# Attention logits: from TensorE matmuls to a copy of k through memory, a VectorE transpose and a ScalarE leaky ReLU

## Chip, core and metric

One core of one Trainium2 chip runs the whole program. The metric is device time in microseconds. Before the change it is 1596.43 us, the median of three runs (1595.44 to 1596.8).

## The reference

128 graphs, each with 128 nodes of 256 features (float32) and its own 128x128 adjacency. Layer 0 is a graph convolution, layer 1 graph attention with 8 heads. The change is in the lines of `logits` and `masked`:

```python
h  = relu(layernorm(x))                       # layer 0
x  = x + adj @ (h @ weight) + bias
h2 = relu(layernorm(x))                       # layer 1
fp = (h2 @ fc_w + fc_b)                       # 8 heads of 256
q, k = fp @ q_w + q_b, fp @ k_w + k_b         # one number per node and head
logits = q + transpose(k)                     # 128 x 128 per head
masked = leaky_relu(logits + (1 - adj) * -1e9, 0.01)
attn = softmax(masked)
out = sigmoid((attn @ fp) @ fp_w + fp_b + h2)
x = x + out
```

## The kernel before

**Groups and slots.** A group is GB = 4 graphs; there are 32. A hand-written program puts each engine's instructions in order. One group is 44 slots on TensorE: four units (two pairs of graphs times two halves of the heads), each with the 11 entries of ORDER (L590). A "g" entry multiplies the attention by h2 (`aggregate`, L559) into PSUM; a number m is the product of the combined term f[m] with a folded weight (`multiply`, L604), which for a unit stands 11 slots behind its g. `take` (L576 to L585) brings g out of PSUM: ScalarE copies f0, f1 and f3, VectorE makes f4 and f6, GpSimd f5 and f2. So unit 0's f4 is multiplied at slot 16, unit 2's f3 at slot 34. `combine` (L620 to L639) puts a pair's results together on VectorE.

**PLAN.** The list PLAN (L665) says after which slot other work is put into the engines' queues, as (slot, group relative to the current one, function). Each engine runs its own queue in order; an entry's slot fixes that order, and an engine can be ahead of TensorE's slot or behind. In the time of group g, group g+1 goes through its softmax, g+2 gets its second layer norm, its transposed h2 (`turn_h2_blocks`, L435) and q and k, and g+3 goes through layer 0: `first_a` (L372, copied out by ScalarE at L379) at slot 35, `first_b` (L388, with VectorE's add at L395) at slots 37 and 40. The statistics (L290, L291) and `rdev_both` (L302 on VectorE, L306 on GpSimd) follow; the normalization itself is a ScalarE ReLU with scale and bias per node (L324). Group g-1 gets its sigmoid (L652), `finish` (L656) and the store.

**Logits.** `make_qk` computes q and k of a group for all heads as rows: 32 rows for each graph, 8 of q, 8 of k, 16 empty (L459). `left` (L467) and `kr` (L469) hold these rows with ones put in, and `right` (L471, GpSimd) spreads `kr` over the heads, zero but for the own head. One matmul per graph and half of the blocks, with 32 rows in the contraction, then gives q + k for 128x512 at once in PSUM:

```python
nc.tensor.matmul(lp, lhsT=s["left"][ts(b, Q), :], rhs=s["right"][ts(b, Q), js],
                 start=True, stop=True)
```

`logits` (L486) runs at slots 1 and 4, four matmuls each. `masked` (L499) adds the mask on VectorE, from PSUM into the tile `attn`; `head_max` (L511) applies the leaky ReLU as max(0.01 a, a) and takes the negative maximum per head (L513). `exps` (L521) is one ScalarE Exp per head, with the maximum as bias and the sum read out. `normal` scales by the reciprocal (L529 on VectorE, L530 on GpSimd). `move` (L541) sends 32-row blocks of attn to other partitions, 16 DMAs a pair, all in SyncE's queue, and `turn` (L548) transposes them in 32x32 blocks on VectorE. SyncE's queue also holds the moves of h2 (L431), the loads (L67, L69, L77) and the output (L657). Matmuls write to the six PSUM buffers of ps_m.

Before the first group, a setup folds the weights and takes groups 0 and 1 through the same steps by hand; FIRST_PLAN adds what is missing in the first group.

Of the kernel before, what the change touches and what calls it, by code (L numbers as in the profile page):

```python
# [9 lines left out]
FP = mybir.dt.float32  # L10
# [8 lines left out]
H = 8  # L19
# [9 lines left out]
def gnn_then_gat_kernel(  # L29
# [31 lines left out]
    small = ctx.enter_context(tc.tile_pool(name="small", bufs=3))  # L61
    ps_m = ctx.enter_context(tc.tile_pool(name="ps_m", bufs=6, space=PSUM))
# [42 lines left out]
    mq = const.tile([P, 1], FP, name="mq")  # L105
    mk = const.tile([P, 1], FP, name="mk")
    lb = const.tile([P, 1], FP, name="lb")
    rb = const.tile([P, 1], FP, name="rb")
    heads = const.tile([P, H], FP, name="heads")
# [29 lines left out]
    cols = sp.tile([P, ROWS], FP, name="cols")  # L139
    ones = sp.tile([P, P], FP, name="ones")  # L140
# [6 lines left out]
    def setup_rows():  # L147
# [23 lines left out]
        nc.vector.tensor_tensor(heads, rows[:, 0:H], rows[:, H : 2 * H], ALU.add)  # L171
# [52 lines left out]
    def setup_bias():  # L224
# [253 lines left out]
    def logits(s, half, bs=range(GB)):  # L478
# [3 lines left out]
        js = ts(half, NB // 2)  # L482
        for b in bs:
            lp = ps_m.tile([P, NB // 2, H, Q], FP, name="logits", tag="m")
            s["l", half, b] = lp
            nc.tensor.matmul(  # L486
                lp,
                lhsT=s["left"][ts(b, Q), :],
# [309 lines left out]
    for half in range(2):  # L798
        n1_apply(s1, half)
# [153 lines left out]
```

## Time and profile before

| What | Value |
|---|---|
| median of the runs | 1596.43 us |
| the profiled execution: time, and its span | 1593.71 us, 1591.9 us |
| its mean granted TensorE clock | 0.987 |
| a steady stretch of 96 us (302 to 398): clock; busy PE, DVE, ACT, POOL | 1.00; 96.00, 82.96, 56.49, 70.50 us |
| DMA queue of SyncE: share of 16 engines | 35.4% |
| idle of VectorE before L499, put down to the logits | 137.3 us in 61 waits |
| idle of ScalarE before the Exp, put down to the maximum | 95.4 us in 65 waits |

The steady stretch is two groups and a little. A group of instructions is told by its line, engine and operation, output and inputs, then the shape, the count, the busy time in us and the mean of one in ns, and at the end the idle time of the engine before them with what ended it. A timeline row is its start in us, its length, and the same names. float32 matmuls leave two records each. PE is TensorE, DVE VectorE, ACT ScalarE, POOL GpSimd, SP SyncE.

### The profile page before, as it was taken

The numbers are of one execution on the slowest core, as the hardware profiler recorded it, in microseconds if no ns is written. First come the engines' busy times: TensorE is split into PE (matmuls) and PEld (weight loads), VectorE is DVE, ScalarE is ACT, GpSimd is POOL, SyncE is SP. The second block draws the span as 40 slices with busy tenths as digits, with TensorE's granted clock in tenths as the row PEclk, the third lists the DMA queues.
The fourth block names the chain that finished last, engine by engine and source line by source line (L and its number), as shares of the span: only waits on it lengthen the run. The fifth ranks groups of instructions, "written<-read, shape, count | busy, mean of one in ns | idle before, by whom it ended". The sixth has DMA issues, their size and how long they took to land.

```text
span 1591.9 us, 30601 instructions
## 1 busy us (share of the span) xinstructions
PE 1564.3 (98%) x10433; PEld 1229.5 (77%) x10433; DVE 1313.2 (82%) x2352; ACT 888.2 (56%) x2865; POOL 1112.5 (70%) x756
## 2 busy tenths in 40 slices
PE   7989999999999999999999999999999999999997
PEld 6667777877777877777777777887777787777776
DVE  5888888988888998888898888898888898887762
ACT  3554556665555665555666555666555666555551
POOL 2465778766678766677866677876667876667774
PEclk7899999999999999999999999999999999999999
DMA  5233334333334433333433333433333443323220
GB/s 179 53 81 87 84 90 100 91 83 92 90 82 98 98 89 84 90 79 97 102 88 86 87 80 95 102 91 83 90 91 82 99 96 86 89 71 78 70 67 27
DMA packets 236644, 139.44 MB, mean 88 GB/s; under 512 B 151860, under 2 KB 203464, under 8 KB 236232
## 3 DMA queue, kind: packets, MB, share of 16 engines
q1 hardware_dynamic: 236248, 137.16, 35.4%
q8 instruction: 82, 1.34, 0.4%
q14 instruction: 74, 0.61, 0.1%
q10 hardware_dynamic: 240, 0.33, 0.1%
HBM read 37.76 MB, written 16.78 MB: 34 GB/s over the span
## 4 chain that ended last, share of the span: by engine, by line
PE 93%; DVE 2%; DMA 1%; issue 1%; POOL 1%; ACT 1%; SPq 0%; POOLq 0%; DVEq 0%
PE acc L604 51%; PE g_ps L559 28%; PE x_ps L388 6%; PE logits L486 4%; PE ah_ps L372 3%; PE qk_ps L459 1%; DMA fpw<-in_L_gnn_fp_w_dram 1%; DVE attn L499 0%; ACT attn L521 0%; DMA b_bc<-in_L_gnn_bias_dram 0%; DVE attn L511 0%; DVE attnT L548 0%; DVE st L290 0%; DVE nmax L513 0%; ACT h L324 0%
## 5 line engine op out<-in xcount | busy, mean ns | idle before, releaser
L604 PEld LDWEIGHTS acc<-wts,f 128*128 128x128 f32 x7168 | 895.6, 192 | 296.1 <-issue 255.4
L604 PE MATMUL acc<-wts,f 128*128 128x128 f32 x7168 | 909.6, 276 | 3.9 <-ACT f L584 3.9
L559 PE MATMUL g_ps<-attnT,h 128*128 128x512 f32 x1024 | 529.4, 599 | 4.3 <-DVE attnT L548 4.3
L521 ACT ACTIVATE attn<-attn,nmax 128x128 f32<-128x128 f32 x1024 | 397.5, 391 | 96.2 <-DVE nmax L513 95.4
L582 POOL TENSOR_TENSOR f<-f,f 128x512 f32<-128x512 f32 x128 | 193.3, 1510 | 298.6 <-DVE f L580 294.1
L530 POOL TENSOR_TENSOR attn<-attn,total 128x1024 f32<-128x1024 f32 x128 | 277.8, 2170 | 40.9 <-DVE total L529 40.9
L584 ACT COPY f<-g_ps 128x512 f32<-128x512 f32 x128 | 73.6, 575 | 382.9 <-PE g_ps L559 231.3
L499 DVE TENSOR_TENSOR attn<-logits,mask 128x512 f32<-128x512 f32 x256 | 159.0, 683 | 137.3 <-PE logits L486 137.3
L511 DVE SCALAR_TENSOR_TENSOR attn<-attn 128x1024 f32<-128x1024 f32 x128 | 207.5, 1621 | 0.0
L585 POOL TENSOR_TENSOR f<-f,f 128x512 f32<-128x512 f32 x128 | 188.9, 1476 | 8.9 <-ACT f L584 3.9
L521 ACT ACTIVATION_READ_ACCUMULATOR attn<-attn,nmax 128x1 f32 x1024 | 193.1, 189 | 0.0
L548 DVE STREAM_TRANSPOSE attnT<-attnB 128x1024 f32<-128x1024 f32 x128 | 154.5, 1226 | 14.2 <-DMA attnB<-attn 13.8
L559 PEld LDWEIGHTS g_ps<-attnT,h 128*128 128x128 f32 x1024 | 155.8, 192 | 13.1 <-issue 10.1
L513 DVE TENSOR_REDUCE nmax<-attn 128x8 f32<-128x1024 f32 x128 | 156.2, 1220 | 4.4
L578 ACT COPY f<-g_ps 128x512 f32<-128x512 f32 x128 | 73.5, 574 | 115.5 <-PE g_ps L559 115.5
L648 POOL TENSOR_TENSOR z<-z,h 128x256 f32<-128x256 f32 x128 | 90.5, 727 | 51.7 <-DVE z L620 44.1
L388 PE MATMUL x_ps<-w_sb,ahT 128*128 128x256 f32 x512 | 121.0, 380 | 0.0
L620 DVE TENSOR_TENSOR z<-w,v 128x256 f32<-128x256 f32 (+1 forms) x128 | 116.2, 947 | 2.2
L388 PEld LDWEIGHTS x_ps<-w_sb,ahT 128*128 128x128 f32 x512 | 93.0, 191 | 11.0 <-issue 1.0
L576 ACT COPY f<-g_ps 128x512 f32<-128x512 f32 x128 | 73.6, 575 | 41.9 <-PE g_ps L559 40.7
L580 DVE TENSOR_TENSOR f<-g_ps,f 128x512 f32<-128x512 f32 x128 | 85.8, 670 | 8.2 <-PE g_ps L559 6.1
L581 DVE TENSOR_TENSOR f<-f,g_ps 128x512 f32<-128x512 f32 x128 | 86.5, 676 | 0.0
(95 smaller groups left out, 1444.6 us busy)
## 6 DMA issues: line engine op xcount, KB each, us to landing
attnB<-attn SPq DMA_DIRECT2D x1019, 64.0 KB, 2.0
xg<-in_x_dram SPq DMA_DIRECT2D x32, 512.0 KB, 4.1
out_dram<-z SPq DMA_DIRECT2D x31, 512.0 KB, 2.9
h2B<-h SPq DMA_DIRECT2D x480, 32.0 KB, 1.9
ag<-in_adj_dram SPq DMA_DIRECT2D x32, 256.0 KB, 4.7
agB<-in_adj_dram SPq DMA_DIRECT2D x120, 64.0 KB, 4.3
fcw<-in_L_gnn_fc_w_dram SPq DMA_DIRECT2D x2, 1024.0 KB, 7.2
fpw<-in_L_gnn_fp_w_dram SPq DMA_DIRECT2D x1, 2048.0 KB, 14.1
```

The source lines that it names most:

```text
L388: nc.tensor.matmul(op[:, bb, :], lhsT=s["ahT"][:, 2 * b2 + bb, c, :], rhs=w0_sb[:, c, :], start=(c == 0), stop=(c == NC - 1),)
L499: nc.vector.tensor_tensor(s["a", b // 2][:, js, b % 2], s["l", half, b], s["mask"][:, b, :] .rearrange("p (j c) -> p j c", c=Q)[:, js] .un ...
L511: nc.vector.scalar_tensor_tensor(a, a, 0.01, a, ALU.mult, ALU.max)
L513: nc.vector.tensor_reduce(nmax, a.rearrange("p j h c -> p h j c"), AX.XY, ALU.max, negate=True)
L521: nc.scalar.activation(a[:, :, h, :], a[:, :, h, :], AF.Exp, bias=s["nmax", b][:, h : h + 1], accum_out=s["total", b][:, h : h + 1],)
L530: nc.gpsimd.tensor_tensor(a, a, total.unsqueeze(1).unsqueeze(3).to_broadcast([P, NB, H, Q]), ALU.mult)
L548: nc.vector.transpose(aT.rearrange("p h (i r) -> p i h r", r=Q), s["ab", b // 2][:, :, b % 2])
L559: nc.tensor.matmul(u["g", b, c], lhsT=s["h2"][:, 2 * pair + b].rearrange("p j c q -> p (j c q)")[:, ts(c, P)], rhs=s["aT", 2 * pair + b][: ...
L582: nc.gpsimd.tensor_tensor(new(5), f[4], f[0], ALU.subtract)
L585: nc.gpsimd.tensor_tensor(new(2), f[1], f[5], ALU.subtract)
L604: nc.tensor.matmul(acc[:, slot, :], lhsT=u["f"][m][:, h, :], rhs=wt[m][:, half * HU + h, :], start=(half == 0 and h == 0 and m in FIRST), ...
L620: nc.vector.tensor_tensor(o, a, b, ALU.add)
```

## The change

`left`, `right` and `logits` go, with their PLAN entries. `make_qk` adds the bias to the rows (`qk`). `turn_qk` transposes them on TensorE, so that nodes lie on partitions, copies k and q out on VectorE and stores k (128 x 32 numbers) to a buffer in memory. `load_k` reads it back four times, each into 32 partitions, so that each block of 32 partitions holds all of k. `spread` is VectorE's 32x32 transpose with an input in which each number is repeated 32 times, so that its output holds k along the row in every partition. `masked` is that and then one mask add over 128x1024, in place in SBUF. `leaky` is one ScalarE Prelu per head, with q as its bias and slope 0.01; `head_max` keeps just the maximum. The PLAN moves: the softmax steps start at slot 0, the Exp run in eights, the moves of attn are split (8, 8, 6, 10) around the store and the loads of k, make_qk stands at slot 24 instead of 30, add_b0 behind finish instead of before it, and the output's DMA is split off from finish (`store`). In the setup the same steps take the place of the logits of groups 0 and 1.

```diff
--- before.py
+++ after.py
@@ -59,6 +59,7 @@
     gp = ctx.enter_context(tc.tile_pool(name="group", bufs=2))
     at = ctx.enter_context(tc.tile_pool(name="attention", bufs=2))
     small = ctx.enter_context(tc.tile_pool(name="small", bufs=3))
+    mem = ctx.enter_context(tc.tile_pool(name="mem", bufs=2, space=bass.MemoryType.DRAM))
     ps_m = ctx.enter_context(tc.tile_pool(name="ps_m", bufs=6, space=PSUM))
     ps_o = ctx.enter_context(tc.tile_pool(name="ps_o", bufs=1, space=PSUM))
 
...
@@ -232,12 +230,9 @@
                 start=(kk == 0),
                 stop=(kk == NC - 1),
             )
-        bias = sp.tile([P, 1], FP, name="bias")
         both = sp.tile([P, 1], FP, name="both")
         nc.vector.scalar_tensor_tensor(both, mq, qkb[:, 0:1], bp, ALU.mult, ALU.add)
-        nc.vector.scalar_tensor_tensor(bias, mk, qkb[:, 1:2], both, ALU.mult, ALU.add)
-        nc.vector.scalar_tensor_tensor(lb, bias, mq, mk, ALU.mult, ALU.add)
-        nc.vector.scalar_tensor_tensor(rb, bias, mk, mq, ALU.mult, ALU.add)
+        nc.vector.scalar_tensor_tensor(qk_bias, mk, qkb[:, 1:2], both, ALU.mult, ALU.add)
 
 
 
...
@@ -463,52 +457,63 @@
                     start=(c == 0),
                     stop=(c == NC - 1),
                 )
-        s["left"] = gp.tile([P, P], FP, name="left", tag="left")
-        nc.vector.tensor_scalar(s["left"], qk, mq, lb, ALU.mult, ALU.add)
-        kr = small.tile([P, P], FP, name="kr", tag="kr")
-        nc.vector.tensor_scalar(kr, qk, mk, rb, ALU.mult, ALU.add)
-        s["right"] = gp.tile([P, NB, H, Q], FP, name="right", tag="right", bufs=1)
-        nc.gpsimd.tensor_tensor(
-            s["right"],
-            heads.unsqueeze(1).unsqueeze(3).to_broadcast([P, NB, H, Q]),
-            kr.rearrange("p (j c) -> p j c", c=Q).unsqueeze(2).to_broadcast([P, NB, H, Q]),
-            ALU.mult,
-        )
-
-    def logits(s, half, bs=range(GB)):
-
-
-
-        js = ts(half, NB // 2)
-        for b in bs:
-            lp = ps_m.tile([P, NB // 2, H, Q], FP, name="logits", tag="m")
-            s["l", half, b] = lp
-            nc.tensor.matmul(
-                lp,
-                lhsT=s["left"][ts(b, Q), :],
-                rhs=s["right"][ts(b, Q), js],
-                start=True,
-                stop=True,
-            )
-
-    def masked(s, half, bs=range(GB)):
-        js = ts(half, NB // 2)
-        for b in bs:
-            if half == 0 and b % 2 == 0:
-                s["a", b // 2] = at.tile([P, NB, 2, H, Q], FP, name="attn", tag="attn", bufs=3)
-            nc.vector.tensor_tensor(
-                s["a", b // 2][:, js, b % 2],
-                s["l", half, b],
-                s["mask"][:, b, :]
-                .rearrange("p (j c) -> p j c", c=Q)[:, js]
-                .unsqueeze(2)
-                .to_broadcast([P, NB // 2, H, Q]),
-                ALU.add,
+        s["qk"] = gp.tile([P, P], FP, name="qk", tag="qk", bufs=1)
+        nc.vector.tensor_scalar(s["qk"], qk, qk_bias, None, ALU.add)
+
+    def turn_qk(s):
+
+
+        tp = ps_m.tile([P, GB, Q], FP, name="q_ps", tag="m")
+        nc.tensor.transpose(tp.rearrange("p b r -> p (b r)"), s["qk"], ident)
+        k = small.tile([P, GB, H], FP, name="k", tag="k", bufs=2)
+        nc.vector.tensor_copy(k, tp[:, :, H : 2 * H])
+        s["q"] = gp.tile([P, GB, H], FP, name="q", tag="q")
+        nc.vector.tensor_copy(s["q"], tp[:, :, 0:H])
+        s["k_mem"] = mem.tile([P, GB * H], FP, name="k_mem", tag="k_mem")
+        nc.sync.dma_start(s["k_mem"], k.rearrange("p b h -> p (b h)"))
+
+    def load_k(s):
+        s["kq"] = gp.tile([P, NB, GB, H], FP, name="kq", tag="kq")
+        for n in range(NB):
+            nc.sync.dma_start(
+                s["kq"][ts(n, Q)].rearrange("r j b h -> r j (b h)"),
+                s["k_mem"].rearrange("(j r) c -> r j c", r=Q),
+            )
+
+
+
+    def spread(s, b):
+
+        if b % 2 == 0:
+            s["a", b // 2] = at.tile([P, NB, 2, H, Q], FP, name="attn", tag="attn", bufs=3)
+        nc.vector.transpose(
+            s["a", b // 2][:, :, b % 2],
+            s["kq"][:, :, b].unsqueeze(3).to_broadcast([P, NB, H, Q]),
+        )
+
+    def masked(s, b):
+        spread(s, b)
+        a = s["a", b // 2][:, :, b % 2]
+        nc.vector.tensor_tensor(
+            a,
+            a,
+            s["mask"][:, b, :]
+            .rearrange("p (j c) -> p j c", c=Q)
+            .unsqueeze(2)
+            .to_broadcast([P, NB, H, Q]),
+            ALU.add,
+        )
+
+    def leaky(s, b, h0=0, nh=H):
+        a = s["a", b // 2][:, :, b % 2]
+        for h in range(h0, h0 + nh):
+            nc.scalar.activation(
+                a[:, :, h, :], a[:, :, h, :], AF.Prelu,
+                bias=s["q"][:, b, h : h + 1], alpha=0.01,
             )
 
     def head_max(s, b):
         a = s["a", b // 2][:, :, b % 2]
-        nc.vector.scalar_tensor_tensor(a, a, 0.01, a, ALU.mult, ALU.max)
         nmax = s["nmax", b] = small.tile([P, H], FP, name="nmax", tag="nmax", bufs=4)
         nc.vector.tensor_reduce(
             nmax, a.rearrange("p j h c -> p h j c"), AX.XY, ALU.max, negate=True
@@ -654,6 +659,9 @@
     def finish(s, b0, nb):
         bs = slice(b0, b0 + nb)
         nc.gpsimd.tensor_tensor(s["z"][:, bs], s["z"][:, bs], s["x1"][:, bs], ALU.add)
+
+    def store(s, b0, nb):
+        bs = slice(b0, b0 + nb)
         nc.sync.dma_start(
             out[GB * s["g"] + b0 : GB * s["g"] + b0 + nb].rearrange("b n d -> n b d"),
             s["z"][:, bs],
@@ -664,67 +672,71 @@
 
     PLAN = [
         (0, "u", take, 0, 0, 0),
-        (1, 1, logits, 0),
-        (1, 1, masked, 0),
+        (0, 1, masked, 0),
+        (0, 1, masked, 1),
+        (0, 1, leaky, 0),
         (2, 2, shift_both),
         (3, "u", take, 0, 1, 1),
         (3, 2, n2_apply, 0),
         (3, 2, n2_apply, 1),
         (3, 2, move_h2),
-        (4, 1, logits, 1),
-        (4, 1, masked, 1),
+        (4, 1, leaky, 1),
+        (4, 1, head_max, 0),
+        (5, 1, masked, 2),
         (6, "u", combine, -1, 4),
-        (6, 1, head_max, 0),
+        (7, "u", take, 0, 1, 0),
+        (7, 1, head_max, 1),
         (8, 4, begin),
         (8, 3, load_blocks),
-        (8, "u", take, 0, 1, 0),
         (9, "u", take, 0, 0, 1),
-        (9, 1, exps, 0, 0, 4),
-        (10, 1, head_max, 1),
-        (11, "u", take, 1, 0, 0),
+        (9, 1, exps, 0, 0, 8),
         (11, "u", combine, -1, 2),
         (11, -1, residual_b, 1),
-        (11, 1, exps, 0, 4, 4),
+        (11, "u", take, 1, 0, 0),
+        (11, 1, leaky, 2),
         (12, 0, turn, 2),
+        (12, 1, masked, 3),
         (12, 1, normal, 0),
-        (13, 1, exps, 1, 0, 1),
-        (13, 1, head_max, 2),
+        (13, 0, turn, 3),
         (14, "u", take, 1, 1, 1),
-        (14, 1, exps, 1, 1, 3),
-        (15, 1, exps, 1, 4, 4),
-        (16, 0, turn, 3),
-        (17, 1, normal, 1),
+        (14, 1, head_max, 2),
+        (14, 1, exps, 1, 0, 8),
         (17, "u", take, 1, 1, 0),
-        (17, 1, exps, 2, 0, 4),
-        (18, 1, exps, 2, 4, 2),
-        (19, 1, head_max, 3),
+        (18, 2, turn_h2_blocks),
+        (18, 1, normal, 1),
+        (18, 1, move, 0, range(8)),
         (20, "u", take, 1, 0, 1),
-        (20, 1, exps, 2, 6, 2),
-        (20, 1, move, 0),
+        (20, 1, leaky, 3),
+        (20, 1, head_max, 3),
+        (20, 1, exps, 2, 0, 8),
         (21, 0, residual_a, 0),
-        (22, 1, normal, 2),
         (22, "u", take, 2, 0, 0),
         (22, 1, exps, 3, 0, 4),
-        (24, 3, n1_apply, 0),
+        (24, 2, make_qk),
         (25, "u", take, 2, 1, 1),
+        (25, 1, normal, 2),
+        (25, 1, exps, 3, 4, 4),
+        (25, 3, n1_apply, 0),
         (25, 3, n1_apply, 1),
-        (26, 1, exps, 3, 4, 4),
-        (26, 2, turn_h2_blocks),
         (27, "u", combine, 1, 4),
+        (28, "u", take, 2, 1, 0),
+        (27, 2, turn_qk),
+        (28, 1, move, 0, range(8, 16)),
+        (28, 1, normal, 3),
         (28, 3, turn_blocks),
         (28, 4, n1_stats, 0),
-        (28, "u", take, 2, 1, 0),
         (28, 4, n1_stats, 1),
-        (28, 3, add_b0),
         (28, -1, sigmoid, 0, GB),
         (29, -1, finish, 0, GB),
-        (30, 1, normal, 3),
-        (30, 2, make_qk),
+        (29, 3, add_b0),
+        (30, 1, move, 1, range(6)),
         (31, "u", take, 2, 0, 1),
         (32, "u", combine, 1, 2),
         (32, 0, residual_b, 0),
         (33, "u", take, 3, 0, 0),
-        (33, 1, move, 1),
+        (34, 2, load_k),
+        (34, 1, move, 1, range(6, 16)),
+        (34, -1, store, 0, GB),
         (34, 1, turn, 0),
         (34, 1, turn, 1),
         (35, 3, first_a, 0),
@@ -741,7 +753,7 @@
         (43, 0, residual_a, 1),
     ]
 
-    LATE = (shift_both, n2_apply, move_h2, turn_h2_blocks, make_qk)
+    LATE = (shift_both, n2_apply, move_h2, turn_h2_blocks, make_qk, turn_qk, load_k, turn)
 
     groups = [{"g": g} for g in range(NG)]
     pool = {}
@@ -795,6 +807,8 @@
     turn_h2(s0, 1)
     setup_wqk(1)
     make_qk(s0, wqk_p)
+    turn_qk(s0)
+    load_k(s0)
     for half in range(2):
         n1_apply(s1, half)
     turn_adj(s1)
@@ -802,17 +816,17 @@
     add_b0(s1)
     for half in range(2):
         n1_stats(s2, half)
-    logits(s0, 0, (0, 1))
-    logits(s0, 1, (0, 1))
-    masked(s0, 0, (0, 1))
-    masked(s0, 1, (0, 1))
     first_a(s1, 0)
     first_a(s1, 1)
+    masked(s0, 0)
+    leaky(s0, 0)
+    masked(s0, 1)
+    leaky(s0, 1)
+    first_b(s1, 0)
+    first_b(s1, 1)
     head_max(s0, 0)
     exps(s0, 0, 0, H)
     head_max(s0, 1)
-    first_b(s1, 0)
-    first_b(s1, 1)
     exps(s0, 1, 0, H)
     setup_weights(0, 0, True)
     normal(s0, 0)
@@ -835,35 +849,37 @@
     setup_weights(4, 1, True)
     make_qk(s1, wqk_p)
     setup_wqk_order()
-    logits(s0, 0, (2, 3))
-    masked(s0, 0, (2, 3))
-    logits(s0, 1, (2, 3))
-    masked(s0, 1, (2, 3))
+    masked(s0, 2)
     for h in range(5, H):
         setup_weights(h, 0, False)
         setup_weights(h, 1, False)
-    head_max(s0, 2)
-    setup_sums(0)
-    setup_fpb()
-    exps(s0, 2, 0, H)
+    leaky(s0, 2)
+    masked(s0, 3)
+    leaky(s0, 3)
+    turn_qk(s1)
+    load_k(s1)
     turn(s0, 0)
     turn(s0, 1)
+    head_max(s0, 2)
+    setup_fpb()
+    setup_sums(0)
+    exps(s0, 2, 0, H)
     setup.close()
     pool["un"] = ctx.enter_context(tc.tile_pool(name="unit", bufs=2))
     FIRST_PLAN = [
         (0, load_blocks, s2),
         (1, begin, s3),
+        (1, turn_blocks, s2),
         (1, normal, s0, 2),
         (1, head_max, s0, 3),
         (1, n1_apply, s2, 0),
         (1, n1_apply, s2, 1),
         (2, exps, s0, 3, 0, H),
         (2, add_b0, s2),
-        (2, turn_blocks, s2),
         (6, normal, s0, 3),
         (6, move, s0, 1),
-        (6, first_a, s2, 0),
-        (6, first_a, s2, 1),
+        (4, first_a, s2, 0),
+        (4, first_a, s2, 1),
         (7, setup_sums, 1),
         (7, make_mask, s2),
         (7, n1_stats, s3, 0),
...
```

More of the change, by code (lines that the diff above doesn't have):

```diff
@@ L102, in gnn_then_gat_kernel @@
     nc.gpsimd.memset(wqk_p, 0.0)
[L105 to L109, printed above, removed]
+    qk_bias = const.tile([P, 1], FP, name="qk_bias")
     setup = ExitStack()
@@ L139, in gnn_then_gat_kernel @@
     cols = sp.tile([P, ROWS], FP, name="cols")
+    mq = sp.tile([P, 1], FP, name="mq")
+    mk = sp.tile([P, 1], FP, name="mk")
     ones = sp.tile([P, P], FP, name="ones")
@@ L170, in setup_rows @@
         nc.vector.tensor_reduce(mk, rows[:, H : 2 * H], AX.X, ALU.add)
-        nc.vector.tensor_tensor(heads, rows[:, 0:H], rows[:, H : 2 * H], ALU.add)
     def setup_turn(c):
@@ L883, in gnn_then_gat_kernel @@
         (38, make_qk, s2),
+        (40, turn_qk, s2),
+        (40, load_k, s2),
+        (41, turn, s1, 0),
+        (41, turn, s1, 1),
     ]
@@ L902, in gnn_then_gat_kernel @@
             for at_, who, f, *args in PLAN:
-                if at_ != slot or (g == 0 and (f in LATE or (f is turn and who == 0))):
+                if at_ != slot or (g == 0 and f in LATE):
                     continue
@@ L914, in gnn_then_gat_kernel @@
                 finish(cur, 0, 2)
+                store(cur, 0, 2)
     for o in ORDER:
@@ L921, in gnn_then_gat_kernel @@
     finish(cur, 2, 2)
+    store(cur, 2, 2)
 _INS = [
```

## The prediction

> **What bounds the kernel now.** I read the page's busy shares and its chain that ended last, then the stretch of one group, the chain inside it, the groups by line, and the engines' timelines.
>
> ```profile
> span 1591.9 us, 30601 instructions
> ...
> PE 1564.3 (98%) x10433; PEld 1229.5 (77%) x10433; DVE 1313.2 (82%) x2352; ACT 888.2 (56%) x2865; POOL 1112.5 (70%) x756
> ...
> PE acc L604 51%; PE g_ps L559 28%; PE x_ps L388 6%; PE logits L486 4%; PE ah_ps L372 3%; PE qk_ps L459 1%; DMA fpw<-in_L_gnn_fp_w_dram 1%; DVE attn L499 0%; ACT attn L521 0%; DMA b_bc<-in_L_gnn_bias_dram 0%; DVE attn L511 0%; DVE attnT L548 0%; DVE st L290 0%; DVE nmax L513 0%; ACT h L324 0%
> ```
>
> TensorE carries the chain: from 110 to 1550 us it never stops. The logits, 4% of the chain, are work that the change deletes. The chain passes the same logits at 794.67 and at 841.97 us: one group takes 47.30 us. The busy times of that stretch, engine by engine, show what stands behind TensorE:
>
> ```profile
> core 0: us, PE busy (x) PEld busy (x) DVE busy (x) ACT busy (x) POOL busy (x), PEclk, DMA share, GB/s
> 794.67:841.97 47.30, 47.30 (x324) 37.16 (x324) 40.80 (x72) 27.55 (x89) 34.57 (x24) 1.00 0.37 90
> ```
>
> The chain of waits around one logits step (start, us, what):
>
> ```profile
> 841.08 0.89 PE acc L604 x8
> 841.97 1.07 PE logits L486 x8
> 843.04 1.09 PE acc L604 x8
> ```
>
> Four logits matmuls cost 1.07 us, and the products behind them 1.09 where 0.89 is usual: 1.27 us a step, two steps a group, **2.54 us**.
>
> **The change, part by part.** *TensorE.* It loses 2.54 us a group and gains one 128x128 transpose. In the setup 32 such transposes (L178) took 3.66 us, 0.11 each; a switch behind the narrow qk_ps tiles costs the next product 0.19. I take 0.2: 47.30 - 2.34 = **44.96 us**, if nobody else makes it wait. The bounds are 0.11 and 0.3.
>
> *VectorE.* The rows that price it:
>
> ```profile
> L499 DVE TENSOR_TENSOR attn<-logits,mask 128x512 f32<-128x512 f32 x256 | 159.0, 683 | 137.3 <-PE logits L486 137.3
> L511 DVE SCALAR_TENSOR_TENSOR attn<-attn 128x1024 f32<-128x1024 f32 x128 | 207.5, 1621 | 0.0
> L548 DVE STREAM_TRANSPOSE attnT<-attnB 128x1024 f32<-128x1024 f32 x128 | 154.5, 1226 | 14.2 <-DMA attnB<-attn 13.8
> ```
>
> Removed per group: 8 x 0.683, 4 x 1.621, and left and kr (0.364 + 0.403): 12.7 us. Added: 4 spreads at the 1.226 of L548 (a repeated input is shown nowhere; below, the 1.19 of L435's transposes; above, I allow 1.8, half as much again), 4 mask adds over 128x1024, one add of 128x128 (0.36), two small copies (0.17 each, as L198). The mask add now has two SBUF inputs, as L511 has, and L511's instructions run from 1.167 to 2.005 us. The timeline says why:
>
> ```profile
> 853.80 1.92 DVE L511 SCALAR_TENSOR_TENSOR attn<-attn 128x1024 f32<-128x1024 f32 x1
> ...
> 853.37 1.27 POOL L582 TENSOR_TENSOR f<-f,f 128x512 f32<-128x512 f32 x1 [9.40 <-DVE f L580]
> 854.72 2.14 POOL L585 TENSOR_TENSOR f<-f,f 128x512 f32<-128x512 f32 x1
> ```
>
> GpSimd runs until 854.64, VectorE then takes its 1.1 us, and GpSimd's next one stretches from 1.27 to 2.14: they take turns. The Trainium skill (SBUF — State Buffer, "SBUF: two separate sides") has the rule: a Vector op with two SBUF inputs and a GpSimd op hold a shared port pair one at a time. It speaks against moving L499's add from PSUM into SBUF: the rule alone would add up to 4 x 0.45 us of waiting. But L511, with the same size and lock, leaves. So the row prices the mask adds at 4 x 1.17 to 4 x 1.62. The sum added is 10.3 to 12.1 us, VectorE falls from 40.8 to 38.4-40.2 of 45, and GpSimd loses `right` (1.91).
>
> *ScalarE* takes over the leaky ReLU: 32 Prelu a group, 128x128, bias per partition. The nearest row is the Exp, same size and bias, with a readout of its sum:
>
> ```profile
> 806.18 0.40 ACT L521 ACTIVATE attn<-attn,nmax 128x128 f32<-128x128 f32 x1
> 806.48 0.19 ACT L521 ACTIVATION_READ_ACCUMULATOR attn<-attn,nmax 128x1 f32 x1
> 806.58 0.39 ACT L521 ACTIVATE attn<-attn,nmax 128x128 f32<-128x128 f32 x1
> ...
> 839.42 0.58 ACT L584 COPY f<-g_ps 128x512 f32<-128x512 f32 x1 [8.16 <-PE g_ps L559]
> ```
>
> An Exp takes 0.39 but frees the engine after 0.295; Prelu has no readout. I take 0.295 (range 0.29 to 0.39): 8 are 2.36 us, 32 are **9.4 us**. ScalarE goes from 27.55 to 37.0 of 45. The skill (ScalarE: Activation LUTs, "Rules for kernel authors") says to keep relu-like work on VectorE; that would cost VectorE 6.5 us (4 x 1.621) instead of these 9.4. The total fits; but ScalarE's work stands in a fixed order, and its slack lies at the end of a group (the 8.16 above). Table loads stay two a group: in the built order none stands at a Prelu.
>
> *DMA.* Per group, one store of k (16 KB) and four loads (16 KB each, 128-byte rows) join SyncE's queue, 60 issues instead of 55. From the page, us to landing last:
>
> ```profile
> attnB<-attn SPq DMA_DIRECT2D x1019, 64.0 KB, 2.0
> ...
> out_dram<-z SPq DMA_DIRECT2D x31, 512.0 KB, 2.9
> ...
> agB<-in_adj_dram SPq DMA_DIRECT2D x120, 64.0 KB, 4.3
> ```
>
> Issues follow at 0.66 to 0.72 us (16 attnB in 10.59 and 11.52), so the five cost 3.3 to 3.6. The store (2.9 to land) has 14 attnB issues, over 9 us, between it and the loads: hidden. The store itself waits for a copy on VectorE at about s+28, and SyncE comes to it at s+29.5 (below): nothing behind it is held up. The loads land in 2.0 to 4.3 us. Behind them wait ten attnB, the output and h2B; the attnB of pair 1 is wanted 12 slots into the next group, so they have time.
>
> *New waits.* VectorE's first maximum now waits for ScalarE's first leaky ReLU, to about s+5.2. Behind it stand the third spread and mask add and f4 and f6, which are done by s+11 with it; TensorE wants f4 at slot 16, 14 us into the group. The first leaky ReLU in turn waits for VectorE's first spread: that is s+2.8 below. Of TensorE's PSUM tiles eight go and one comes; I price that at nothing, since no wait of TensorE for them is among the page's.
>
> **Who is late next.** I follow the order from the start s of a group's first spread. *Round trip A*: spread 1.16, mask add 1.17 and 0.45 of waiting for GpSimd's rstd: s+2.8. ScalarE then has, without a gap, up to the end of its sigmoid: 4 leaky 9.4, 4 times eight Exp at 0.385 12.3, seven copies at 0.47 3.3, eight layer norms (L324) at 0.5 4.0, two table loads 2.6, sigmoid 1.0: 32.6, s+35.4. GpSimd's finish and add_b0 (2.4 + 2.36): s+40.2. VectorE's two x1 adds, their statistics, f4 and f6 between, rstd (0.68+1.1+1.2+0.68+1.1+0.24): **s+45.2**, and the next spread starts. *Round trip B*: the second batch's Exp end at s+21.3 (s+2.8, three leaky 7.1, two times Exp 6.2, four copies 1.9, four layer norms 2.0, one table load 1.3), its reciprocal and its scaling on GpSimd (1.91) at s+24; SyncE issues 8 attnB, k, 14 attnB, 4 loads: 27 x 0.66 to 0.72 = 17.8 to 19.4; landing 2.0 to 4.3: **s+43.8 to s+47.7**. Both circle back to the spread within a microsecond of TensorE's 44.96. So TensorE's gain is not all to be had: I take 45.5 us a group (45.2 and 0.3 for turns at the shared port), 1.8 less than 47.30.
>
> **Sum.** 30 full periods x 1.8 = 54. The first group stalls on ScalarE and transposes already (1.97 and 3.91 us idle); removing its logits gives perhaps 1. In the setup k's way through memory (store 2.9, four issues 2.5, landing 2 to 4.3) is some 4 us longer than right and logits, but the turns there stand earlier in VectorE's order: +2. Against the profiled execution's 1593.71: 1593.7 - 54 - 1 + 2 = 1540.7. The median 1596.43 is 2.7 above it: **1543 us**.
>
> **Rivals.**
> - *TensorE stays the only bound* (25%): mask adds at 1.17, GpSimd out of the way, no gap of TensorE. 30 x 2.34 = 70: 1596.4 - 70 + 1 = 1527, and 1519 if the setup gives back its two logits steps (3.78 and 1.99 us) instead of losing 2. For it: 98% busy now. Against: ScalarE's gap-free 32.6.
> - *k arrives late* (17%): round trip B at about 46, loads landing near 3: 1596.4 - 39 + 1 = 1558; at 4.3 and the slow issue pace 47.3 is passed. For it: every load from memory shown takes 4 us or more; against: these are small.
> - *Slower: ScalarE becomes the bound* (15%). Place: the 32 Prelu of round trip A. If they don't overlap (0.39 each), it is 45.2 + 3.0 + 0.3 = 48.5, 1.2 above today: 1596 + 36 + 1 = 1633. It decides from 0.36 each on (2.1 us over 32). A spread at 1.8 instead of 1.2 adds only its own 0.6 to the round trip.
> - *It does nothing* (3%): the waits eat just the 2.3.
>
> The likeliest case, A, has 40%: 1530 to 1560. The range, 1517 to 1590, holds A, the first rival and most of the second. Faster by over 0.2% (about what a measurement of this kernel can tell from no change): A, the first rival, and 0.15 of the second: 0.80; within 0.2%: 0.04; slower: 0.16.
>
> **What would show it.** The group's period between two make_qk steps: 45.5, or 45.0, or above 47.3. Prelu in steps of 0.295; spreads of 1.2; mask adds of 1.17 to 1.9; ScalarE's gap before slot 36 gone; TensorE idle, a few tenths a group, before products with f of the third unit or before x_ps, released by ScalarE. If the first spread of a group waits for the kq load, round trip B decides. Wrong I would be if TensorE stayed without gaps, or if Prelu or the spread cost more than the rows they are priced by.

## The result, and the profile after

The changed kernel takes 1575.07 us (median of four runs, 1573.85 to 1576.38) against 1595.93 for the kernel before in the same comparison: ratio 0.987, 95% interval 0.985 to 0.989, some 21 us less. The forecast was 1543, 53 us less; 1575 lies inside its range (1517 to 1590), but not where its likeliest case was put (1530 to 1560). The sign came true and the new bound is of the kind that was forecast; the gain is less than half of the forecast. The two profiled executions, 1593.71 and 1576.38 us, lie somewhat closer together, with 17.7 us between their spans.

The page after, busy times and the chain that ended last, by engine and by line (L526 is the Exp, L510 the leaky ReLU, L609 the products with the weights):

```profile
PE 1509.0 (96%) x9953; PEld 1213.2 (77%) x9953; DVE 1228.9 (78%) x2253; ACT 1173.8 (75%) x3889; POOL 984.0 (63%) x724
...
ACT 44%; PE 23%; DVE 16%; SPq 9%; issue 4%; DMA 2%; POOL 2%; ACTq 0%; POOLq 0%; DVEq 0%
ACT attn L526 18%; PE acc L609 11%; ACT attn L510 10%; SPq L546 6%; DVE attn L497 6%; ACT h L319 6%; PE x_ps L383 5%; PE g_ps L564 5%; DVE attn L489 5%; ACT f L589 2%; ACT L657 2%; ACT L526 2%; SPq L426 2%; ACT z L657 2%; DVE st L285 1%
```

Before, some 93% of this chain was TensorE. Now ScalarE holds 44% of it and TensorE 23%. TensorE is still 96% busy, but it waits in every group. So the bound has moved from an engine to a round trip through several.

The sigmoids (one per group) are good milestones, since they stand at the same place of the order in both kernels. Their starts in the two timelines, in us:

| | before | after | difference |
|---|---|---|---|
| first sigmoid | 165.07 | 180.44 | +15.4 |
| the 27 periods behind it | 1277.30 (47.31 each) | 1247.10 (46.19 each; 46.11 mostly) | -30.2 |
| the last four groups, shorter | 144.38 | 141.53 | -2.9 |
| to the end of the span | 5.15 | 5.13 | 0.0 |
| span | 1591.9 | 1574.2 | -17.7 |

Two things are off: the start-up loses 15 us where +1 was forecast, and a period gains 1.1 us where 1.8 was.

**The start-up.** The timeline after around group 2's first spread, rows of SyncE, VectorE and TensorE (start, length, instruction, and in brackets the idle time before it with its releaser; SPq is SyncE's queue, and L473 and L478 are the store and the loads of k):

```profile
119.73 22.15 SPq L546 DMA_DIRECT2D attnB<-attn  x32
141.99 0.53 SPq L473 DMA_DIRECT2D k_mem<-k  x1
143.63 1.73 SPq L478 DMA_DIRECT2D kq<-k_mem  x4
146.83 1.25 DVE L489 STREAM_TRANSPOSE attn<-kq 128x1024 f32<-128x1024 f32 x1 [11.07 <-DMA kq<-k_mem]
156.48 3.76 PE L609 MATMUL acc<-wts,f 128*128 128x128 f32 x16 [11.04 <-DVE z L625]
```

VectorE has k ready at 129.9, but its store stands in SyncE's queue behind 32 moves of attn, which all come due at once here (in the steady plan they are split around it). Store and loads follow at 142.0 and 143.6, VectorE waits 11.07 us for them, ScalarE waits for VectorE, and TensorE stands still for 11.04 us. The windows of the same trace (busy us of each engine, then the granted TensorE clock) show what this costs besides:

```profile
core 0: us, PE busy (x) PEld busy (x) DVE busy (x) ACT busy (x) POOL busy (x), PEclk, DMA share, GB/s
...
156.40:160.00 3.60, 3.52 (x16) 3.55 (x17) 3.53 (x7) 3.60 (x18) 2.55 (x2) 0.50 0.31 49
160.00:164.00 4.00, 4.00 (x22) 2.88 (x21) 3.97 (x6) 4.00 (x15) 1.56 (x3) 0.83 0.31 50
```

TensorE comes back at half clock: 16 matmuls take 3.76 us, later 1.95, and the two behind them take 1.70 instead of 1.02. That is 2.5 us more. The Trainium skill (TensorE: Matmul & The Clock Gate, Part 1) states half rate after idling until some 3.4 us of activity; the 0.50 of these 3.6 us agrees.

**The period.** The round trip in a steady group of the changed kernel, from its timeline, in order of time:

```profile
827.84 1.06 ACT L657 ACTIVATE z<-z 128x1024 f32<-128x1024 f32 x1
...
828.80 0.57 ACT L589 COPY f<-g_ps 128x512 f32<-128x512 f32 x1
828.98 2.37 POOL L661 TENSOR_TENSOR z<-z,x 128x1024 f32<-128x1024 f32 x1 [1.96 <-ACT z L657]
...
829.42 1.16 PE L609 MATMUL acc<-wts,f 128*128 128x128 f32 x8 [0.40 <-ACT f L589]
...
831.29 2.36 POOL L337 TENSOR_TENSOR xg<-xg,b_bc 128x1024 f32<-128x1024 f32 x1
...
833.69 0.69 DVE L390 TENSOR_TENSOR x<-x_ps,xg 128x512 f32<-128x512 f32 x1 [1.25 <-POOL xg L337]
...
834.87 1.89 PE L383 MATMUL x_ps<-w_sb,ahT 128*128 128x256 f32 x8
...
836.80 0.69 DVE L390 TENSOR_TENSOR x<-x_ps,xg 128x512 f32<-128x512 f32 x1
...
838.92 1.25 DVE L489 STREAM_TRANSPOSE attn<-kq 128x1024 f32<-128x1024 f32 x1
...
840.68 1.88 POOL L590 TENSOR_TENSOR f<-f,f 128x512 f32<-128x512 f32 x1
...
841.46 2.45 ACT L510 ACTIVATE attn<-attn,q 128x128 f32<-128x128 f32 x8 [0.52 <-DVE attn L497]
...
842.52 1.27 POOL L648 TENSOR_TENSOR h<-h,fpb_j 128x512 f32<-128x512 f32 x1
842.62 2.26 DVE L497 TENSOR_TENSOR attn<-attn,mask 128x1024 f32<-128x1024 f32 x1
...
844.80 0.22 DVE L308 SCALAR_TENSOR_TENSOR nb<-mv,rstd 128x4 f32<-128x4 f32 x2
...
844.98 2.08 ACT L319 ACTIVATE h<-x,nb,rstd 128x256 f32<-128x256 f32 x4 [0.60 <-DVE nb L308]
```

Sigmoid (L657), finish (L661), add_b0 (L337), the first x1 add (L390), the spread, the leaky ReLU: each begins where the one before it ends, but for the statistics, f4 and f6 and the second x1 add, which fill VectorE between the x1 add and the spread. That is round trip A, link by link.

Two things were not followed in the forecast. The first is a second branch that is just as long. ScalarE's copy of f (L589) stands behind the sigmoid, TensorE waits 0.40 us for it, and its x_ps for the second x1 add ends at 836.76; VectorE comes to that add from its own work at 836.78. The chain of the page takes the branch through TensorE, and GpSimd has only 2% of it. The prediction named such a wait of TensorE as a sign, but not as a branch of the round trip. By these times, shortening GpSimd's branch alone would gain next to nothing.

The second is a wait. The second mask add (842.62) takes 2.26 us instead of 1.23, because GpSimd's L590 and L648 run until 843.79; it ends 1.09 us after them, so this is a turn at the shared port. `nb` (L308), two tiny instructions that make the bias of the layer norms, stands behind it, and ScalarE waits 0.60 us for `nb` ahead of the layer norms. The round trip against the forecast:

| link | forecast | measured |
|---|---|---|
| first spread to first leaky ReLU | 2.8 | 2.54 |
| leaky ReLU to the end of the sigmoid | 32.6 | 33.55, of which 0.60 idle |
| end of the sigmoid to the x1 add | 4.8 | 4.79 |
| x1 add to the next spread | 5.0 | 5.23 |
| sum | 45.2, 45.5 with 0.3 for the port | 46.11 |

The clock is no part of this: from 200 to 1400 us the granted TensorE clock is 1.00 in both traces.

### The profile page after: what moved, and what is told of

Its sections match the earlier page's. It is cut to its first block, busy times and chain, and to the rows that moved or that the text cites. A ratio compares the mean times of both kernels' runs of the same rounds, so it can differ in the third digit from the quotient of the medians.

```text
span 1574.2 us, 30745 instructions
## 1 busy us (share of the span) xinstructions
PE 1509.0 (96%) x9953; PEld 1213.2 (77%) x9953; DVE 1228.9 (78%) x2253; ACT 1173.8 (75%) x3889; POOL 984.0 (63%) x724
## 3 DMA queue, kind: packets, MB, share of 16 engines
q8 instruction: 78, 1.28, 0.4%
## 4 chain that ended last, share of the span: by engine, by line
ACT 44%; PE 23%; DVE 16%; SPq 9%; issue 4%; DMA 2%; POOL 2%; ACTq 0%; POOLq 0%; DVEq 0%
ACT attn L526 18%; PE acc L609 11%; ACT attn L510 10%; SPq L546 6%; DVE attn L497 6%; ACT h L319 6%; PE x_ps L383 5%; PE g_ps L564 5%; DVE attn L489 5%; ACT f L589 2%; ACT L657 2%; ACT L526 2%; SPq L426 2%; ACT z L657 2%; DVE st L285 1%
## 5 line engine op out<-in xcount | busy, mean ns | idle before, releaser
L609 PEld LDWEIGHTS acc<-wts,f 128*128 128x128 f32 x7168 | 889.6, 192 | 281.2 <-issue 181.7
L609 PE MATMUL acc<-wts,f 128*128 128x128 f32 x7168 | 897.9, 276 | 23.8 <-DVE z L625 12.9
L526 ACT ACTIVATE attn<-attn,nmax 128x128 f32<-128x128 f32 x1024 | 397.3, 396 | 0.4
L587 POOL TENSOR_TENSOR f<-f,f 128x512 f32<-128x512 f32 x128 | 163.2, 1275 | 286.7 <-DVE f L585 284.4
L510 ACT ACTIVATE attn<-attn,q 128x128 f32<-128x128 f32 x1024 | 312.9, 391 | 34.4 <-DVE attn L497 27.1
L535 POOL TENSOR_TENSOR attn<-attn,total 128x1024 f32<-128x1024 f32 x128 | 245.1, 1915 | 140.8 <-DVE total L534 140.8
L589 ACT COPY f<-g_ps 128x512 f32<-128x512 f32 x128 | 73.3, 572 | 241.1 <-PE g_ps L564 241.1
L526 ACT ACTIVATION_READ_ACCUMULATOR attn<-attn,nmax 128x1 f32 x1024 | 199.3, 195 | 0.0
L497 DVE TENSOR_TENSOR attn<-attn,mask 128x1024 f32<-128x1024 f32 x128 | 186.4, 1456 | 4.5
L590 POOL TENSOR_TENSOR f<-f,f 128x512 f32<-128x512 f32 x128 | 180.5, 1410 | 6.5 <-ACT f L589 3.9
L553 DVE STREAM_TRANSPOSE attnT<-attnB 128x1024 f32<-128x1024 f32 x128 | 153.3, 1218 | 39.7 <-DMA attnB<-attn 34.7
L489 DVE STREAM_TRANSPOSE attn<-kq 128x1024 f32<-128x1024 f32 x128 | 157.2, 1228 | 15.9 <-DMA kq<-k_mem 15.6
L661 POOL TENSOR_TENSOR z<-z,x 128x1024 f32<-128x1024 f32 (+1 forms) x33 | 76.2, 2310 | 56.3 <-ACT z L657 56.3
L581 ACT COPY f<-g_ps 128x512 f32<-128x512 f32 x128 | 74.0, 578 | 40.7 <-PE g_ps L564 39.6
```

The costliest lines, as they stand in the source:

```text
L489: nc.vector.transpose(s["a", b // 2][:, :, b % 2], s["kq"][:, :, b].unsqueeze(3).to_broadcast([P, NB, H, Q]),)
L497: nc.vector.tensor_tensor(a, a, s["mask"][:, b, :] .rearrange("p (j c) -> p j c", c=Q) .unsqueeze(2) .to_broadcast([P, NB, H, Q]), ALU.add,)
L510: nc.scalar.activation(a[:, :, h, :], a[:, :, h, :], AF.Prelu, bias=s["q"][:, b, h : h + 1], alpha=0.01,)
L526: nc.scalar.activation(a[:, :, h, :], a[:, :, h, :], AF.Exp, bias=s["nmax", b][:, h : h + 1], accum_out=s["total", b][:, h : h + 1],)
L535: nc.gpsimd.tensor_tensor(a, a, total.unsqueeze(1).unsqueeze(3).to_broadcast([P, NB, H, Q]), ALU.mult)
L553: nc.vector.transpose(aT.rearrange("p h (i r) -> p i h r", r=Q), s["ab", b // 2][:, :, b % 2])
```

## The experiments

The theory: the period is round trip A, drawn out by the wait for `nb`; the start-up loss is SyncE's queue. Rivals: TensorE or SyncE's k (round trip B) set the period; the start-up loss is the setup itself. A period below is the median spacing of the sigmoids over the 27 full periods, from each run's trace. All edits are to the changed kernel, except that of e4_logits_twice, which is to the kernel before.

| run | what | ratio to before (95%) | period, us |
|---|---|---|---|
| | the change itself | 0.987 (0.985 to 0.989) | 46.11 |
| e1_first_k | k of group 2 through ScalarE's queue | 0.980 (0.978 to 0.981) | 46.10 |
| e2_shift_early | `nb` ahead of the second mask add | 0.977 (0.976 to 0.979) | 45.41 |
| e9_two_moves | both | 0.970 (0.968 to 0.971) | 45.42 |
| e6_one_leaky_less | one leaky ReLU of four left out | 0.971 (0.970 to 0.972) | 45.01 |
| e3_bias_first | add_b0 before finish | 0.994 (0.992 to 0.995) | 46.44 |
| e5_sigmoid_late | sigmoid behind ScalarE's next copies | 1.004 (1.003 to 1.006) | 47.04 |
| e7_three_moves | e1, e2 and e5 | 0.988 (0.986 to 0.989) | 46.47 |
| e8_five_moves | e7, with `nb` between the second spread and its mask add, and make_qk a slot later | 0.985 (0.983 to 0.986) | 46.33 |
| e10_late_x1_5 | e5, and five buffers for x1 | 0.975 (0.974 to 0.976) | 45.37 |
| e11_five_moves_x1_5 | e8, and five buffers for x1 | 0.960 (0.959 to 0.962) | 44.89 |
| e12_no_table_loads | e9, the sigmoid as a tanh | 0.970 (0.969 to 0.972) | 45.32 |
| e4_logits_twice | the kernel before, logits issued twice | 1.036 (1.035 to 1.038) | 49.02 (before: 47.31) |

**The start-up: k of group 2 by another queue.** Only group 2's store and loads move, from SyncE's queue to ScalarE's; `turn_qk` and `load_k` get the queue as an argument (not shown).

```diff
-        (40, turn_qk, s2),
-        (40, load_k, s2),
+        (40, turn_qk, s2, nc.scalar),
+        (40, load_k, s2, nc.scalar),
```

> The changed kernel, with the store and the loads of k of group 2 alone (the first group's time) issued from ScalarE's queue instead of SyncE's, where they stood behind 32 moves of attn until 141.99 us. Theory 1 (the first group loses 11.07 us of VectorE's wait for kq and some 2.5 us of TensorE at a lower clock after it): 1575 - 11 to - 14 = 1561 to 1564 us, the period of a group stays 46.1. Rival (other waits of the first two groups take its place, the moves of pair 1 above all): 1570 to 1575.

Measured: 1561.8 us, 13 less than the change (12 by the two ratios), as theory 1 expected. The same place in this kernel's timeline (SyncE's 32 moves still run from 121.45 for 23.90 us):

```profile
130.97 0.36 ACTq L473 DMA_DIRECT2D k_mem<-k  x1
132.57 1.78 ACTq L478 DMA_DIRECT2D kq<-k_mem  x4
...
136.67 1.24 DVE L489 STREAM_TRANSPOSE attn<-kq 128x1024 f32<-128x1024 f32 x1
```

The store leaves as soon as k is there, the spread starts 10 us earlier with no wait, and the longest gap of TensorE here is under 1 us. The first sigmoid comes at 170.3 (180.4 before this edit), and the period is unchanged: 10 us of the loss were the queue, once. The other 5 us against 165.1 stay; 2.1 are the setup (first product with attention at 74.70 instead of 72.62), as forecast, and the other 3 were not followed.

**The period: `nb` ahead of the second mask add.**

```diff
         (0, 1, masked, 0),
+        (0, 2, shift_both),
         (0, 1, masked, 1),
         (0, 1, leaky, 0),
-        (2, 2, shift_both),
```

> The changed kernel with shift_both put ahead of the second mask add in VectorE's order (slot 0, after the first mask add), so that ScalarE's layer norms no longer wait behind a mask add that waits for GpSimd. Theory 1 (a round trip ScalarE, GpSimd, VectorE sets the period, and its 0.60 us gap before the layer norms is in it): the period falls from 46.13 to 45.5 to 45.6, the time by 28 x 0.6 = 17 us to 1558. Rival (the waits for memory or TensorE itself set the period): within 3 us of 1575.

Measured: 1558.04, as theory 1 expected. Rows of its timeline:

```profile
831.77 1.30 DVE L308 SCALAR_TENSOR_TENSOR nb<-mv,rstd 128x4 f32<-128x4 f32 x2
...
834.71 2.08 ACT L319 ACTIVATE h<-x,nb,rstd 128x256 f32<-128x256 f32 x4
```

`nb` now does the waiting (1.30 instead of 0.22; it ends just behind GpSimd's L590, which runs until 832.99), but ahead of the time at which ScalarE wants it. The layer norms start without a wait, and the second mask add, from 834.26, takes 1.23 us, since GpSimd's L648 ends at 834.22. The period falls by 0.70, a little more than the 0.60 that ScalarE had waited: this wait lay on the path in full.

**Both**, to see whether they add:

> The changed kernel with k of the first group from ScalarE's queue and with shift_both ahead of the second mask add, and nothing else. The two losses lie in different stretches (the first group; every group), so theory 1 expects them to add: 1575 - 13 - 17 = 1545 us, the period 45.45 as with shift_both alone. If they share a cause: 1551 or more.

1546.81. In ratios 0.0074 and 0.0098 make 0.0172 together, measured 0.0174: they add.

**Is it ScalarE's queue at all, and where is TensorE's floor?** The leaky ReLU of one graph of four is left out:

```diff
-        (20, 1, leaky, 3),
```

> The changed kernel without the leaky ReLU of the fourth graph of each group in the steady program (q and the slope are left out for it), so ScalarE has 2.35 us less to do in the stretch that theory 1 calls gap-free. Theory 1: the round trip falls by 2.35 to 43.8, and the period to the next limit, 45.0 to 45.4: 1552 to 1545. Rival (VectorE's and GpSimd's turns at the port set the period): within 3 us of 1575.

1548.73. ScalarE has 2.35 us less to do, the period falls by 1.10 and stops at 45.01 in most groups. So ScalarE's queue is in the round trip, and another limit lies close below. It is not yet TensorE alone (forecast 44.96), as a row of this trace shows:

```profile
711.31 0.67 PE L453 MATMUL qk_ps<-h2T,wqk 128*32 128x128 f32 x16 [0.20 <-DVE h2T L430]
```

TensorE still waits here for VectorE's transpose of h2. From the second x1 add VectorE's queue takes 24.6 us to the end of that transpose, and from make_qk TensorE takes 20.3 us to the next second x1 add: 45.0 together, a round trip without ScalarE that the prediction did not have.

**The order of add_b0 and finish.** The change put GpSimd's add_b0 behind finish. If the x1 add waits only for add_b0, taking that first should help.

```diff
+        (28, 3, add_b0),
         (28, -1, sigmoid, 0, GB),
         (29, -1, finish, 0, GB),
-        (29, 3, add_b0),
```

> The changed kernel with add_b0 ahead of finish in GpSimd's order, as it was before the change, so that VectorE's add of x1 doesn't wait for the sigmoid. Theory 1a (the round trip closes through GpSimd alone): the period falls by 1.2 to TensorE's 44.96, 1541 us. Theory 1b (a second branch closes nearly as late: ScalarE's copy of f behind the sigmoid holds up TensorE, whose x_ps ends at 836.60 while VectorE starts its add at 836.80): the period falls by 0.2 at most, to 45.95, 1570 us. Rival (GpSimd's order does not matter): 1575.

A miss for all the expectations: 1584.8, 10 slower than the change. Its timeline, GpSimd and VectorE (narrow windows, which show the two z adds apart):

```profile
833.02 2.36 POOL L337 TENSOR_TENSOR xg<-xg,b_bc 128x1024 f32<-128x1024 f32 x1
...
834.30 1.35 DVE L625 TENSOR_TENSOR z<-w,v 128x256 f32<-128x256 f32 x1
...
835.33 2.54 POOL L661 TENSOR_TENSOR z<-z,x 128x1024 f32<-128x1024 f32 x1
...
835.58 2.44 DVE L625 TENSOR_TENSOR z<-w,v 128x128 f32<-128x128 f32 x1
```

add_b0 and finish now run one right behind the other over VectorE's two z adds, which take 3.72 us together instead of 0.62 (at 828.27 in the change): the first ends 0.27 us behind add_b0, the second 0.15 behind finish. The transposes of attn (`turn`) and the x1 add stand behind them: the x1 add comes 5.3 us behind the end of the sigmoid instead of 4.8. The Trainium skill (SBUF — State Buffer, "SBUF: two separate sides") calls the shared port pair an exclusive lock, held for a whole instruction. The rows agree: the two engines take turns, and each of VectorE's short adds waits out one of GpSimd's long sums. So the run does not tell what the order alone is worth; by the tie of the two branches above it would be little.

**The sigmoid moved out of the round trip.** The sigmoid is not wanted until the output. Put behind ScalarE's next copies, it should leave the round trip.

```diff
-        (28, -1, sigmoid, 0, GB),
-        (29, -1, finish, 0, GB),
-        (29, 3, add_b0),
+        (28, 3, add_b0),
...
-        (34, -1, store, 0, GB),
...
+        (36, -1, sigmoid, 0, GB),
+        (37, -1, finish, 0, GB),
+        (37, -1, store, 0, GB),
```

> The changed kernel with the sigmoid of the group before behind the copies of ahT on ScalarE (slot 36), finish and store at slot 37, and add_b0 ahead of them on GpSimd. Theory 1 (the period is the round trip that runs through the sigmoid: ScalarE's whole queue, then finish and add_b0, or the copy of f behind the sigmoid): both branches lose the sigmoid's 2.3 us, and the next one binds, VectorE's order from the first spread to the transpose of h2 (22.4 us) and TensorE from make_qk to x_ps (20.5 us), about 45.4 in all: 28 x 0.7 = 20 us less, 1555. Rival (ScalarE's total work binds, wherever the sigmoid stands): 1575.

A clear miss: 1602.36, slower than the kernel before. The waits of its trace point to the cause (engine, line, releaser: total us, times, longest):

```profile
DVE x L390 <- POOL z L661: 45.0, 28, 3.4
```

The x1 add waits for *finish* of the group before, 28 times in 32 groups. x1 has four buffers, and the new group's x1 takes the one that finish still reads. Late sigmoid, late finish, late buffer. Two kernels with this move among others missed for the same reason:

> The changed kernel with k of the first group from ScalarE's queue, the sigmoid late, and shift_both ahead of the second mask add. If the gains add where they are of different loops: the first group's 13 us, and a period of 45.0 to 45.4: 1562 - 20 to - 31 = 1531 to 1542. If one limit stands behind all of them (VectorE's order up to the transpose of h2), the period stays at 45.4 as with shift_both alone: 1544.

> As the run with three moves, with shift_both between the second spread and its mask add, so that VectorE doesn't wait for GpSimd's rstd, and make_qk one slot later (25), so that TensorE doesn't wait for VectorE's transpose of h2. If TensorE is then the only bound: 44.96 us a group, 28 x 1.17 less than the run with k of the first group alone: 1562 - 33 = 1529 us. If ScalarE's or the port's waits come back: 1535 or above.

They took 1575.56 and 1570.28, where e9's two moves alone give 1546.81; in both traces the x1 add waits 28 times for finish (38.0 and 35.7 us in all). The test of this reason is one more buffer:

```diff
-            s["x1"] = gp.tile([P, GB, D], FP, name="x1", tag="x1", bufs=4)
+            s["x1"] = gp.tile([P, GB, D], FP, name="x1", tag="x1", bufs=5)
```

> The run with the late sigmoid, with five buffers for x1 instead of four and nothing else. There VectorE's add of x1 waited 1.57 us for finish, which reads the x1 whose buffer it reuses. If that buffer is what made the late sigmoid slow (47.0 us a group): the period falls to 45.4 to 46, 1555 to 1572 us. If the turns at the shared port made it slow: it stays at 1595 to 1602.

1555.46 instead of 1602.36, by this one number: the buffer was the cause. (Its z adds still take 2.64 us beside add_b0, so that was not it.) And all together:

> The run with five moves (46.3 us a group), with five buffers for x1. If only the buffer joined finish to the next round trip, ScalarE and VectorE now run ahead and TensorE alone binds at 45.0 to 45.2: 1531 to 1537 us. If turns at the port are left: 45.5 to 46, 1545 to 1560.

1532.44, the best of the runs, better than the change (0.987) and the kernel before. Its chain from 700 to 850 us:

```profile
by line: PE acc L610 55.3%; PE g_ps L565 30.4%; PE x_ps L383 8.2%; PE ah_ps L367 4.8%; PE qk_ps L453 1.2%; PE q_ps L467 0.3%
```

TensorE is the only bound again, and a period is 44.89 in most groups. Of its moves, make_qk a slot later and the place of `nb` were not run alone with five buffers.

**ScalarE's table loads.** On top of e9: a sigmoid written as 0.5 tanh(x/2) + 0.5 needs no table load between Exp and sigmoid; the factor goes to GpSimd ahead of finish, the constant into the bias that is added anyway.

```diff
-        nc.scalar.activation(z, z, AF.Sigmoid)
+        nc.scalar.activation(z, z, AF.Tanh, scale=0.5)
...
+        nc.gpsimd.tensor_scalar(s["z"][:, bs], s["z"][:, bs], 0.5, None, ALU.mult)
```

> As the run with two moves, with the sigmoid as 0.5 tanh(x/2) + 0.5, the last 0.5 folded into the bias of layer 0 and the first as a scaling on GpSimd ahead of finish, so that ScalarE loads no table in a group (2 x 1.28 us less) and GpSimd has about 1.2 us more. Theory 1 (ScalarE's gap-free queue is in the round trip): the round trip shortens by 1.4 to 2.6 and the period goes to TensorE's 45.0: 1545 - 12 = 1533 us. Rival (VectorE's order alone holds it at 45.45): 1545.

1547.56: no gain over e9 (1546.81), so theory 1's 1533 is missed, and the number is nearer to the rival's 1545. The two loads of 1.28 us are gone from each group, but GpSimd gives them back:

```profile
804.16 2.78 POOL L662 TENSOR_SCALAR z<-z 128x1024 f32<-128x1024 f32 x1 [0.55 <-ACT z L658]
```

The factor was expected at 1.2 us and takes 2.78; finish and add_b0 stand behind it. In the timelines of the two runs ScalarE's stretch from the first leaky ReLU to the end of the sigmoid falls from 32.86 us to 30.03, and the way from there to the first x1 add grows from 4.78 to 7.65. So round trip A is hardly shorter, and the run cannot decide between theory and rival; what free table loads would be worth stays open.

**The price of the logits.** In the kernel before, each four logits matmuls are issued a second time:

```diff
+        for b in list(bs) + list(bs):
             nc.tensor.matmul(
-                lp,
+                s["l", half, b],
```

> The kernel before with each step of four logits matmuls issued twice. It prices what the change took from TensorE. If a step costs 1.27 us as worked out from the chain, 62 steps in the groups add 79 us: 1675, the period 49.8. If the row's neighbours pay (the matmuls overlap better than the chain says), a step adds 1.07 or less: 1660 or below, and the gain was over-counted on TensorE's side.

1652.22, 57.8 more, below the expected 1675 and within the second case, 1660 or below. The chain of that kernel around a step:

```profile
824.28 1.93 PE logits L487 x16
826.21 1.09 PE acc L605 x8
```

A repeat adds 0.86 (1.93 against 1.07): the first matmul's 0.2 and the 0.2 of the products behind it come once a step, not once a repeat. 62 steps of 0.86 are 53, the rest is the setup's. So the run does not say, as the second case has it, that the gain was over-counted: it neither shows nor denies the two times 0.2. The period of e11, 44.89 against 47.30, does: 2.41 gained where 2.34 was forecast.

## Why the prediction was right or wrong, point by point

- *TensorE, 44.96 us without waits*: right. e11 runs at 44.89.
- *VectorE's prices*: right. Spreads mean 1.228 us (1.226 taken), mask adds 1.456 (1.17 to 1.62). In groups of the page after (line, engine, operation, count, busy us, mean ns, idle before):

```profile
L510 ACT ACTIVATE attn<-attn,q 128x128 f32<-128x128 f32 x1024 | 312.9, 391 | 34.4 <-DVE attn L497 27.1
...
L497 DVE TENSOR_TENSOR attn<-attn,mask 128x1024 f32<-128x1024 f32 x128 | 186.4, 1456 | 4.5
...
L489 DVE STREAM_TRANSPOSE attn<-kq 128x1024 f32<-128x1024 f32 x128 | 157.2, 1228 | 15.9 <-DMA kq<-k_mem 15.6
```

- *Prelu at 0.295*: right. One is 0.391 long, eight take 2.45 and free the engine after some 2.35. The rival "ScalarE becomes the bound" needed 0.36 and fell with it.
- *k through memory, hidden in a steady group*: right. Loads land in 1.8 us, and VectorE waits for them three times in the whole run, 11.07 of the 15.6 us in the first group. Round trip B does not set the period, and "k arrives late" as a steady state fell.
- *Round trip A takes TensorE's place*: right in kind. ScalarE's stretch sets the period: e2 and e6 each shorten it and the period with it, and so does e10, which takes the sigmoid out. Two things were missing from it: the branch from the sigmoid through the copy of f and TensorE, as long as GpSimd's here, and the round trip of VectorE and TensorE at 45.0 (e6).
- *"I take 45.5 us a group (45.2 and 0.3 for turns at the shared port)"*: **the first step that failed**, in size. Measured 46.19 over 27 periods (46.11 in most; the first, 47.55, and a few others are longer). The term mis-sized is ScalarE's stretch "without a gap", 32.6: it is 33.55, with a gap of 0.60 and 0.35 more spread over its work; VectorE's 5.0 was 5.23. The prediction allowed the port's delay (0.45) at the first mask add, where it did not fall (1.23 us, while GpSimd's rstd ran from 839.06). It fell on the second, whose delay was priced on VectorE alone; that `nb` stands behind it and ScalarE waits for `nb` was not followed. e2 shows this as the cause of the 0.60. The 0.35 was not tested; e9's stretch, in which ScalarE has no wait, takes 32.86, so most of it seems to be the prices. Cost: 27 x (1.8 - 1.12) = 18.4 us.
- *"removing its logits gives perhaps 1", and "+2" for the setup*: **the second step that failed**. The start-up costs 15.4 instead of 1. The setup's +2 was right. But SyncE's queue was checked for the steady order only ("The store (2.9 to land) has 14 attnB issues, over 9 us, between it and the loads: hidden"); in the first group k stands behind all 32. e1 shows 10 us of the first sigmoid's delay, and 12 to 13 of the time, to be this. Cost against the sum: 14.4 us.
- *"30 full periods"*: 27 and four short groups, whose gain was 2.9 instead of 3 x 1.8 = 5.4. Cost: 2.5 us.
- *The signs*: Prelu in steps of 0.295, the spreads of 1.2 and TensorE's idle tenths released by ScalarE (0.40, above) came. The mask adds go beyond their 1.9 (2.26), and "ScalarE's gap before slot 36 gone" did not come: ScalarE waits there 7.29 us for TensorE, before it was 8.16. The round trip passes through GpSimd, VectorE and TensorE in that time, so the gap could not close.

18.4 + 14.4 + 2.5 = 35.3, which is what lies between the forecast 53 and the span's 17.7. With the two repairs alone (e9) the gain is 48 us, near the forecast. What sets e9's 45.42 no run tests. In its timeline two round trips close at once. One is A: ScalarE has no wait in its 32.86 us, and from the end of the sigmoid to the second x1 add it takes 7.90 us, as in the change. The other is that of VectorE and TensorE, which the profile's chain takes there (24.65 and 20.71 us). As e6 runs this one in 45.0, with less work on ScalarE, A is the likelier cause. e11 goes below it with several moves at once, of which the sigmoid and the x1 buffer are in e10 alone.

## What to carry to other kernels

When a change takes work off the bounding engine and puts it on others, follow the new round trip link by link, with each small instruction that stands behind a slow one in its queue: `nb`, 0.22 us long, cost some 17 us over the run. Check each new DMA in the start-up's order too, and not just in the steady one. When a step is moved later, ask which buffer its last reader holds: one x1 buffer turned a loss of 7 us into a gain of 40 against the kernel before.

## What the runs showed of the hardware that was not expected

- A 32x32 transpose whose input repeats each number 32 times takes 1.228 us, as one with a plain input (L553, 1.218).
- GpSimd's in-place product with a constant over 128x1024 takes 2.78 us, more than its sum of two tensors of that size (2.36), where its mask over 128x512 takes 0.62. Why is open.
- GpSimd's short power (L301, 128x8, 1.65 us) did not delay a mask add that ran beside it (1.23), while two of its larger sums stretched the next one to 2.26.
- Eleven us of idle time cost TensorE 2.5 us more, at a granted clock of 0.50 and then 0.83.
